# A PSUM bank written ahead by ScalarE, and a second diagonal product, in the last group of an edge-gated graph kernel

## The chip, the cores and the metric

One core of one Trainium2 chip runs the whole program in one launch. The metric is the device time of an execution in microseconds (us). The engines are named as the profile names them: PE (TensorE, matrix products; PEld is its weight load), DVE (VectorE), ACT (ScalarE), POOL (GpSimd, which here issues the gathers), SP (SyncE, which issues most other DMAs). SBUF is the on-chip memory that all engines read; PSUM holds the results of products, in banks of 512 fp32 values per partition.

## The reference

`x` is 16 batches of 1024 vertices with 256 features, and `adj` is a sparse 1024 x 1024 matrix (an edge with probability near 0.008, and the diagonal). Cut to what matters, with h = x:

```python
pre_u = h @ W1[:d]; pre_v = h @ W1[d:]
S   = sigmoid(relu(pre_u[u] + pre_v[v] + b1) @ W2 + b2)     # one number per edge (u, v) and batch
a_t = einsum('buv,bud->bvd', S * adj, h)
m_t = einsum('uv,bud->bvd', adj, h) * h
z_t = beta1*h + beta2*(a_t @ Wa + ba) + beta3*(m_t @ Wm + bm)
```

The kernel computes S for the edges alone. `z_t` is the output, and the change concerns how its first term, beta1 h, is added.

## The kernel before, in words

**Tiling.** The vertices v are cut into 8 tiles of 128, the batches into 4 groups g of 4. A pair (g, vt) is a *block*; there are 32, numbered k = 0 to 31 (`order`, L409), and the last group, g = 3, is blocks 24 to 31. A block's edges lie in 10 slots of up to 128 edges; one slot is one *step* n, so there are 320 steps, and s = n mod 10 is the step within its block.

**One step.** POOL gathers 128 rows of 8 KB from `table[g]`, which holds h W1[:d] and h side by side (`fetch`, L515; eight places, `fetched`). PE spreads pre_v over the slot's edges into a PSUM bank pair `pc` (`expand`, L610: two products, issued two steps ahead). DVE adds `pc` to the gathered rows (`add`, L646, one 128x1024 operation, for step n+1), then runs four `scalar_tensor_tensor` with an accumulator for step n (`gate`, L649), which give each edge's score. ACT makes the sigmoid (`gt`, L659) and scales the selection matrices `left` with it (L661). PE multiplies `left` with the gathered h rows into the accumulators `acc` (`aggregate`, L664); this frees the gathered tile, and POOL fetches the next one. At odd steps two slots are aggregated, at even ones none.

**One block's end.** When half of a 64-vertex window is done, ACT copies the accumulator to SBUF (`half_end`, L681), PE transposes it into a bank `misc` (`turn_over`, L691, four transposes) and ACT copies the result to `LT` (L694). For block k this stands in steps 8 and 9 of block k and in steps 0 and 2 of block k+1. DVE multiplies the `m` part with h (L705). Then `block_end(k)` runs in steps 4 to 7 of block k+1, one part to a step, each half (two batches) having two parts:

- steps 4 and 5, first half: a bank `pz` gets the bias row (L719, L449), then eight products with `w_a` in step 4 and eight with `w_m` in step 5 (L722). ACT copies `pz` to SBUF (L736), over the part of `LT` that is used up. One step later DVE makes hb = beta1 hb + z in one `scalar_tensor_tensor` (L737), and one step after that SP sends hb out (L739).
- steps 6 and 7, second half: the same products; in groups 0 to 2 also the same copy and DVE operation. In the last group (`h == 1 and g == NG - 1`, L724) PE adds beta1 h itself: two fp32 products with `be1_eye`, the diagonal matrix of beta1 (L726; the profile counts four, as fp32 goes in two passes). ACT then copies `pz` straight to hb (L728) and SP sends it (L730).

`halves(k+1)` (L473), in steps 1, 3, 4, 6 and 7 of block k, makes pre_v for the next block: a bias row and eight products into a bank (L480, L481), which ACT copies twice, to `X` and to `low` (L482, L483), one half in step 1, the other in step 3; then three copies between halves of the partitions (L486, L489).

**Banks.** `small()` (L220) hands out the two banks of the pool `psm` in turn, to `halves`, `turn_over`, `block_end` and, in the earlier groups, to the rows of the table and the edge lists. A tile that gets a bank waits until the readers of the bank's last tile are done. Block 31 is ended by `tail` (L753).

**Order of the work.** The order on each engine is that in which the program calls (`manual_schedule`, L492). `after(step, f)` puts f in front of the products of a later step. From step `LAST` = 230 on, `expand` and `products` come behind the gate of their step.

Of the kernel before, what the change touches and what calls it, by code (L numbers as in the profile page):

```python
# [7 lines left out]
FP = mybir.dt.float32  # L8
FR = mybir.dt.float32r
I32 = mybir.dt.int32  # L10
AF = mybir.ActivationFunctionType
ALU = mybir.AluOpType
AX = mybir.AxisListType
P = 128
# [3 lines left out]
def kernel(  # L18
# [42 lines left out]
    nc = tc.nc  # L61
    B, N, D = x.shape
    NT = N // P
    DC = D // P
    GB = 4
    NG = B // GB
# [22 lines left out]
    def load_rows(src, n, name, engine=nc.scalar, at_=None):  # L89
        t = const.tile([P, n], FP, name=name) if at_ is None else at_  # L90
        engine.dma_start(t, bass.AP(tensor=src.tensor, offset=src.offset, ap=[[0, P], [1, n]]))
        return t
# [8 lines left out]
    def fixed(shape, name, dt=FP):  # L101
        return const.tile(shape, dt, name=name)
# [90 lines left out]
    bias_p = fixed([P, D], "bias_p", FR)  # L193
# [12 lines left out]
    main = ctx.enter_context(ExitStack())  # L206
# [8 lines left out]
    lst = lst.enter_context(tc.tile_pool(name="lst", bufs=1))  # L215
    psc = main.enter_context(tc.tile_pool(name="psc", bufs=2, space=bass.MemoryType.PSUM))
    psa = main.enter_context(tc.tile_pool(name="psa", bufs=1, space=bass.MemoryType.PSUM))
    psm = main.enter_context(tc.tile_pool(name="psm", bufs=2, space=bass.MemoryType.PSUM))

    def small(name):  # L220
        return psm.tile([P, 512], FP, name="misc")


    def aside(vt):
        return psc.tile([P, GD], FP, name="pc") if vt < EARLY - 1 else small("pl")
# [176 lines left out]
    def after(step, f):  # L402
        due.setdefault(step, []).append(f)
# [38 lines left out]
    def half_product(p, hT, wt, h, begun):  # L442
        for bb in range(2):
            for i in range(DC):
                nc.tensor.matmul(p[:, bb * D:(bb + 1) * D], hT[:, 2 * h + bb, i, :], wt[:, i, :],  # L445
                                 start=(i == 0 and not begun), stop=(i == DC - 1), skip_group_check=begun)

    def add_row(p, parts):
        nc.tensor.matmul(p, unit, parts.unsqueeze(1).to_broadcast([P, 2, D]),  # L449
                         start=True, stop=False, skip_group_check=True)  # L450

    def rows(k, tab=None):

        g, nt = k
        for h in range(2):
            step = yield
            c = slice(2 * h * D, (2 * h + 2) * D)
            p = small("p")
            half_product(p, hTs[k], w_u, h, False)
            t = big.tile([P, 2 * D], FP, name=f"tab{h}", bufs=1) if tab is None else tab[:, c]  # L460
            nc.scalar.copy(t, p)
            if h == 1 and k in again:
                drop_hT(k)
            if tab is None:
                after(step + 1, lambda t=t, c=c: nc.sync.dma_start(table[g][nt * P:(nt + 1) * P, c], t))
        if tab is not None:
            after(step + 1, lambda: nc.sync.dma_start(table[g][nt * P:(nt + 1) * P, :GD], tab))

    cuts = {}

    def halves(k):  # L473
        X = cuts[k] = big.tile([P, NW, GD], FR, name="X")
        low = one.tile([P, GD], FP, name="low")
        for h in range(2):
            step = yield
            c = slice(2 * h * D, (2 * h + 2) * D)
            p = small("p")
            add_row(p, b1_p)  # L480
            half_product(p, hTs[order[k]], w_v, h, True)  # L481
            nc.scalar.copy(X[:, 0, c], p)  # L482
            nc.scalar.copy(low[:, c], p)  # L483
        after(step + (2 if k else 1), lambda: nc.vector.tensor_tensor(low, low, X[:, 0, :].bitcast(FP), ALU.subtract))  # L484
        yield
        nc.scalar.copy(X[W:, 1, :], X[W:, 0, :].bitcast(FP))  # L486
        for w in range(NW):
            yield
            nc.scalar.copy(X[(1 - w) * W:(2 - w) * W, w, :], low[w * W:(w + 1) * W])  # L489
# [56 lines left out]
    marks, pcs, accs, evs, hbs, LTs, lefts = {}, {}, {}, {}, {}, {}, {}  # L546
# [10 lines left out]
    m = 0  # L557
    piece = None
    parts = halves(0)
    for t, turns_ in enumerate(script):  # L560
        step = t - 100
# [148 lines left out]
    def block_end(k):  # L710

        g, vt = order[k]
        hb = hbs[k]
        for h in range(2):
            for i, wt in ((1, w_a), (0, w_m)):
                step = yield
                if i:
                    pz = small("pz")
                    add_row(pz, bias_p)  # L719
                for bb in range(2):  # L720
                    for c in range(DC):
                        nc.tensor.matmul(pz[:, bb * D:(bb + 1) * D], LTs[k][:, 2 * h + bb, i if bb else 1 - i, c, :], wt[:, c, :],  # L722
                                         start=False, stop=(i == 0 and c == DC - 1), skip_group_check=True)
            if h == 1 and g == NG - 1:  # L724
                for bb in range(2):
                    nc.tensor.matmul(pz[:, bb * D:(bb + 1) * D], be1_eye[0], hb[h][:, bb, :], start=False, stop=True,  # L726
                                     skip_group_check=True)
                nc.scalar.copy(hb[h], pz.rearrange("p (b d) -> p b d", b=2))  # L728
                b = g * GB + 2 * h
                after(step + 2, lambda hb=hb[h], b=b: nc.sync.dma_start(  # L730
                    out[b:b + 2, vt * P:(vt + 1) * P, :].rearrange("b p d -> p b d"), hb))
                continue
            z = pz.rearrange("p (b d) -> p b d", b=2)
            if step >= ROOM:
                z = LTs[k][:, 2 * h].rearrange("p k c n -> p (k c n)").rearrange("p (b d) -> p b d", b=2)
                nc.scalar.copy(z, pz.rearrange("p (b d) -> p b d", b=2))  # L736
            after(step + 1, lambda hb=hb[h], z=z: nc.vector.scalar_tensor_tensor(hb, hb, be1, z, ALU.mult, ALU.add))  # L737
            b = g * GB + 2 * h
            after(step + 2, lambda hb=hb[h], b=b: nc.sync.dma_start(  # L739
                out[b:b + 2, vt * P:(vt + 1) * P, :].rearrange("b p d -> p b d"), hb))  # L740
        del hbs[k], LTs[k]
# [79 lines left out]
    def products(n, k, s):  # L821
# [5 lines left out]
        if z <= s < z + 4 and 0 < k < BS:  # L827
            if s == z:
                end = block_end(k - 1)
                next(end)  # L830
            go(end, n)
# [20 lines left out]
        if k + 1 < BS and s - later in (0, 2, 3, 5, 6):  # L852
            if s == later:
                parts = halves(k + 1)
                next(parts)
            go(parts, n)
# [5 lines left out]
    ROOM, MORE, LISTS = 10, 3, 110  # L862
    LAST = (BS - NT - 1) * T
# [18 lines left out]
    for n in range(total + 2):  # L882
        k, s = divmod(n, T)
# [25 lines left out]
        if n == 1:  # L909
            bias = load_rows(bm, D, "bias", nc.sync, spare[:, 1])  # L910
            ba_b = load_rows(ba, D, "ba_b", nc.sync, spare[:, 2])
            be1 = load_rows(beta1, 1, "be1", nc.sync)
# [3 lines left out]
        if s in (5, 7) and k < BS - 1:  # L916
            h = s // 7
            hb = big.tile([P, 2, D], FP, name="h_blk", bufs=4)
            hbs.setdefault(k, []).append(hb)
            g, vt = order[k]  # L920
# [33 lines left out]
    with tc.If(any_left > 0):  # L954
        with ExitStack() as s2:
# [4 lines left out]
            for vt in range(NT):  # L960
                hb = fb.tile([P, B, D], FP, name="fb_h")
# [16 lines left out]
                f = fb.tile([P, 2 * GD], FP, name="fb_f")  # L978
# [3 lines left out]
                with tc.For_i(0, n_turns, 1):  # L982
# [9 lines left out]
                    for g in range(NG):  # L992
                        nc.gpsimd.indirect_dma_start(
                            out=f, out_offset=None, in_=table[g],
# [21 lines left out]
                for b in range(B):  # L1016
# [6 lines left out]
                    pz = fps.tile([P, D], FP, name="fb_pz")  # L1023
                    for k, w in enumerate((w_m, w_a)):
                        for c in range(DC):
                            nc.tensor.matmul(pz, lt[:, k, c, :], w[:, c, :],
                                             start=(k == 0 and c == 0), stop=(k == 1 and c == DC - 1))
# [34 lines left out]
```

## Time and profile before

| what | us |
|---|---|
| median of 3 runs | 1075.63 |
| the three runs | 1077.29, 1075.63, 1071.70 |
| the profiled execution's own time | 1082.24 |
| its span, first to last instruction | 1080.4 |
| busy: PE, DVE, ACT, POOL | 1020.1, 1017.6, 862.6, 459.3 |

The profile is one execution. A row of the timeline gives the start, the duration, the engine, the line of the kernel, the operation, what it writes and reads, and how many instructions are merged. Successive fp32 products overlap: their rows last 379 ns each and start 215 or 216 ns apart, so the distance between starts is what one costs the next. DVE's and ACT's rows overlap in a like way by some 0.07 to 0.12 us. Step 256 (s = 6 of block 25) is where DVE's L737 starts at 885.00 us; the following L737 start at 913.23, 941.42, 969.62, 997.86, 1026.05 and 1053.07, one in each block.

### The profile page before, as it was taken

The numbers are of one execution on the slowest core, as the hardware profiler recorded it, in microseconds if no ns is written. First come the engines' busy times: TensorE is split into PE (matmuls) and PEld (weight loads), VectorE is DVE, ScalarE is ACT, GpSimd is POOL, SyncE is SP. The second block draws the span as 40 slices with busy tenths as digits, with TensorE's granted clock in tenths as the row PEclk, the third lists the DMA queues.
The fourth block names the chain that finished last, engine by engine and source line by source line (L and its number), as shares of the span: only waits on it lengthen the run. The fifth ranks groups of instructions, "written<-read, shape, count | busy, mean of one in ns | idle before, by whom it ended". The sixth has DMA issues, their size and how long they took to land.

```text
span 1080.4 us, 24120 instructions
## 1 busy us (share of the span) xinstructions
PE 1020.1 (94%) x7673; PEld 731.3 (68%) x7673; DVE 1017.6 (94%) x3481; ACT 862.6 (80%) x2616; POOL 459.3 (43%) x456
## 2 busy tenths in 40 slices
PE   7777999999999999999999999999999999999996
PEld 6654676776666776677777767777766667666654
DVE  8687999998999999999999999999999999999993
ACT  3246787788888887898888888889889889999983
POOL 2666676555257334553333334333333333333330
PEclk9989999999999999999999999999999999999999
DMA  9999899999999999999999999999999999999991
GB/s 283 327 340 385 313 339 381 362 382 378 403 352 371 408 381 385 379 403 395 404 393 399 412 384 392 408 396 389 381 361 370 369 348 368 365 381 369 365 341 44
DMA packets 147752, 394.56 MB, mean 365 GB/s; under 512 B 18224, under 2 KB 94512, under 8 KB 111408
## 3 DMA queue, kind: packets, MB, share of 16 engines
q0 software_dynamic: 50544, 301.16, 70.9%
q1 hardware_dynamic: 83776, 78.66, 22.9%
q10 hardware_dynamic: 13296, 13.11, 3.5%
q8 instruction: 63, 1.03, 0.4%
q14 instruction: 73, 0.60, 0.1%
HBM read 396.93 MB, written 50.33 MB: 414 GB/s over the span
## 4 chain that ended last, share of the span: by engine, by line
PE 40%; DVE 34%; issue 10%; ACT 8%; DMA 5%; POOL 2%; another core or an unknown queue 0%; POOLq 0%; DVEq 0%; ACTq 0%
DVE fetched L656 16%; DVE fetched L648 12%; PE acc L673 10%; PE misc L722 10%; PE misc L445 9%; PE pc L615 7%; DMA fetched<-table,uidx 3%; PE misc L691 2%; ACT left L661 2%; DVE LT L705 1%; ACT X L489 1%; PE misc L449 1%; DVE low L484 1%; DVE h_blk L737 1%; DMA hT__635<-in_xT_dram 1%
## 5 line engine op out<-in xcount | busy, mean ns | idle before, releaser
L518 POOL DMA_INDIRECT fetched<-table,uidx x320 | 339.4, 1061 | 529.0 <-PE acc L673 389.0
L656 DVE SCALAR_TENSOR_TENSOR fetched<-fetched,w_b 128x256 f32<-128x256 f32 x1280 | 478.0, 419 | 0.0
L648 DVE TENSOR_TENSOR fetched<-fetched,pc 128x1024 f32<-128x1024 f32 x320 | 387.7, 1212 | 29.9 <-PE pc L615 19.4
L661 ACT ACTIVATE left<-left,gt 128x32 f32<-128x32 f32 (+1 forms) x1280 | 299.6, 305 | 10.4
L673 PE MATMUL acc<-fetched,left 128*32 128x256 f32 x4096 | 273.4, 385 | 6.3 <-ACT gt L659 3.7
L615 PE MATMUL pc<-X,mark 128*128 128x512 f32 x640 | 243.7, 462 | 10.9 <-DVE fetched L648 9.3
L673 PEld LDWEIGHTS acc<-fetched,left 128*32 128x32 f32 x4096 | 127.6, 109 | 112.1 <-issue 29.1
L615 PEld LDWEIGHTS pc<-X,mark 128*128 128x128 f32 x640 | 105.4, 189 | 88.9 <-issue 41.6
L659 ACT ACTIVATE gt<-sc,b_b 128x4 f32<-128x4 f32 x320 | 95.9, 300 | 46.7 <-DVE fetched L656 37.5
L722 PE MATMUL misc<-w_m,LT 128*128 128x256 f32 x496 | 117.3, 379 | 0.0
L722 PE MATMUL misc<-w_a,LT 128*128 128x256 f32 x496 | 117.2, 379 | 0.0
L445 PE MATMUL misc<-w_v,hT 128*128 128x256 f32 x448 | 107.6, 383 | 0.0
L722 PEld LDWEIGHTS misc<-w_a,LT 128*128 128x128 f32 x496 | 93.8, 189 | 15.3 <-issue 0.4
L722 PEld LDWEIGHTS misc<-w_m,LT 128*128 128x128 f32 x496 | 93.8, 190 | 15.1
L625 ACT ACTIVATE left<-onehot,val 128x64 f32<-128x64 bf16 (+1 forms) x320 | 102.9, 322 | 0.0
L385 POOL DMA_INDIRECT val<-in_adjT_dram,vidx x80 | 87.2, 1090 | 34.4 <-issue 20.4
L656 DVE DVE_READ_ACCUMULATOR fetched<-fetched,w_b 128x1 f32 x1280 | 100.7, 79 | 0.0
L691 PE MATMUL misc<-ident,ev 128*128 128x128 f32 x512 | 79.5, 278 | 18.5 <-issue 7.0
L445 PEld LDWEIGHTS misc<-w_v,hT 128*128 128x128 f32 x448 | 86.4, 193 | 14.3
L691 PEld LDWEIGHTS misc<-ident,ev 128*128 128x128 f32 x512 | 60.7, 141 | 45.7 <-ACT ev L681 15.2
L482 ACT CAST X<-misc 128x512 fp32r<-128x512 f32 x64 | 37.1, 580 | 55.2 <-PE misc L445 48.0
L445 PE MATMUL misc<-w_u,hT 128*128 128x256 f32 x320 | 76.6, 386 | 4.0 <-issue 3.8
(185 smaller groups left out, 1011.3 us busy)
## 6 DMA issues: line engine op xcount, KB each, us to landing
h_blk<-table SPq DMA_DIRECT2D x62, 256.0 KB
out_dram<-h_blk SPq DMA_DIRECT2D x62, 256.0 KB
hT<-in_xT_dram SPq DMA_DIRECT2D x28, 512.0 KB
table<-in_x_dram ACTq DMA_DIRECT2D x24, 512.0 KB
table<-tab SPq DMA_DIRECT2D x48, 256.0 KB
fetched<-table,uidx POOLq DMA_INDIRECT x320
table<-in_x_dram SPq DMA_DIRECT2D x8, 512.0 KB
table<-fetched SPq DMA_DIRECT2D x8, 512.0 KB
```

Of the source, the lines that this page charges most:

```text
L385: nc.gpsimd.indirect_dma_start(out=val[:, i, j:j + 1], out_offset=None, in_=adj_flat, in_offset=bass.IndirectOffsetOnAxis(ap=vidx[:, i, j: ...
L445: nc.tensor.matmul(p[:, bb * D:(bb + 1) * D], hT[:, 2 * h + bb, i, :], wt[:, i, :], start=(i == 0 and not begun), stop=(i == DC - 1), skip ...
L518: nc.gpsimd.indirect_dma_start(out=fetched[at_slot[n]], out_offset=None, in_=table[g], in_offset=bass.IndirectOffsetOnAxis(ap=uidx[:, vt * ...
L615: nc.tensor.matmul(pcs[n][:, c], marks[n // TW][:, j * P:(j + 1) * P], cuts[k][:, w, c], start=True, stop=True)
L625: nc.scalar.activation(lefts[n][:, :m, 1::GB, :], onehot[:, i, o:o + m, :].unsqueeze(2).to_broadcast([P, m, GB // 2, V]), AF.Copy, scale=v ...
L648: nc.vector.tensor_tensor(t, t, pcs.pop(n), ALU.add)
L656: nc.vector.scalar_tensor_tensor(t[:, b, :], t[:, b, :], 0.0, w2_b, ALU.max, ALU.mult, accum_out=sc[:, b:b + 1])
L659: nc.scalar.activation(gt, sc, AF.Sigmoid, bias=b2_b)
L661: nc.scalar.activation(lefts[n][:, :m, 2 * b, :], lefts[n][:, :m, 1 + b // 2 * GB, :], AF.Copy, scale=gt[:, b:b + 1])
L673: nc.tensor.matmul(accs[h][b * 2 * V:(b + 1) * 2 * V, r, :], left[:, i, 2 * b - b % 2:2 * b - b % 2 + 2].rearrange("p k v -> p (k v)"), f[ ...
L691: nc.tensor.transpose(pt[:, r, :, c, :], ev[:, r, c * P:(c + 1) * P], ident)
L722: nc.tensor.matmul(pz[:, bb * D:(bb + 1) * D], LTs[k][:, 2 * h + bb, i if bb else 1 - i, c, :], wt[:, c, :], start=False, stop=(i == 0 and ...
```

## The change

The two banks of `psm` get names, and `small` takes a wish for one of them. A new function `seed_z`, called from step 230 on behind the second half of `halves`, takes the bank that this half has just used, keeps it in a list `kept`, and has ACT write beta1 h of the block that ends next (`be1` as the scale) into it. While a bank is kept, `small` hands out the other. `block_end` takes a kept bank for the second half. What `small`, `seed_z`, `halves` and `block_end` get, cut to its core:

```diff
-    psm = main.enter_context(tc.tile_pool(name="psm", bufs=2, space=bass.MemoryType.PSUM))
-    def small(name):
-        return psm.tile([P, 512], FP, name="misc")
+    psm = main.enter_context(tc.tile_pool(name="psm", bufs=1, space=bass.MemoryType.PSUM))
+    turn_of, kept = [0], []
+    def small(name, bank=None):
+        if bank is None:
+            bank = turn_of[0] = 1 - turn_of[0]
+            if kept and kept[0][0] == bank:
+                bank = turn_of[0] = 1 - bank
+        return psm.tile([P, 512], FP, name=f"misc{bank}")
...
-    def add_row(p, parts):
+    def add_row(p, parts, start=True):
...
-                         start=True, stop=False, skip_group_check=True)
+                         start=start, stop=False, skip_group_check=True)
...
+    def seed_z(k, step):
+        bank = turn_of[0]
+        pz = small("pz", bank)
+        kept.append((bank, pz))
+        def write():
+            z, hb = pz.rearrange("p (b d) -> p b d", d=D), hbs[k][1]
+            if step >= LAST:
+                nc.scalar.activation(z, hb, AF.Copy, scale=be1)
...
             nc.scalar.copy(low[:, c], p)
+            if h == 1 and k > 1 and (step >= LAST):
+                seed_z(k - 2, step)
...
                 if i:
-                    pz = small("pz")
-                    add_row(pz, bias_p)
+                    filled = h == 1 and kept
+                    pz = kept.pop()[1] if filled else small("pz")
+                    if not filled or step >= LAST + 6:
+                        add_row(pz, bias_p, not filled)
...
-            if h == 1 and g == NG - 1:
+            by_eye = g == NG - 1 and not filled
+            if by_eye:
                 for bb in range(2):
                     nc.tensor.matmul(pz[:, bb * D:(bb + 1) * D], be1_eye[0], hb[h][:, bb, :], start=False, stop=True,
                                      skip_group_check=True)
+            if by_eye or filled:
                 nc.scalar.copy(hb[h], pz.rearrange("p (b d) -> p b d", b=2))
...
+            else:
+                z = pz.rearrange("p (b d) -> p b d", b=2)
+                if step >= ROOM:
+                    z = LTs[k][:, 2 * h].rearrange("p k c n -> p (k c n)").rearrange("p (b d) -> p b d", b=2)
+                    nc.scalar.copy(z, pz.rearrange("p (b d) -> p b d", b=2))
+                after(step + 1, lambda hb=hb[h], z=z: nc.vector.scalar_tensor_tensor(hb, hb, be1, z, ALU.mult, ALU.add))
```

(The left-out lines of `block_end` are those that send hb out; they stand behind both branches.)

More of the change, by code (lines that the diff above doesn't have):

```diff
@@ L467, in rows @@
             after(step + 1, lambda: nc.sync.dma_start(table[g][nt * P:(nt + 1) * P, :GD], tab))
+    def seed_z(k, step):
[7 more added lines that the diff above has]
+            else:
+                nc.vector.scalar_tensor_tensor(z, hb, be1, bias.unsqueeze(1).to_broadcast([P, 2, D]), ALU.mult, ALU.add)
+        if step >= LAST:
+            write()
+        else:
+            after(step + 1, write)
     cuts = {}
@@ L727, in block_end @@
                                      skip_group_check=True)
+            b = g * GB + 2 * h
+            if by_eye or filled:
                 nc.scalar.copy(hb[h], pz.rearrange("p (b d) -> p b d", b=2))
[L729 to L738, printed above, removed]
+            else:
+                z = pz.rearrange("p (b d) -> p b d", b=2)
[3 more added lines that the diff above has]
+                after(step + 1, lambda hb=hb[h], z=z: nc.vector.scalar_tensor_tensor(hb, hb, be1, z, ALU.mult, ALU.add))
             after(step + 2, lambda hb=hb[h], b=b: nc.sync.dma_start(
```

## The prediction

> **What bounds the kernel now.** I read the page's slices first (PE and DVE at 9 tenths nearly throughout), then the busy time by stretches, since the change acts only from step 230 on.
>
> ```profile
> 740.00:780.00 40.00, 39.87 (x319) 28.94 (x320) 37.59 (x126) 35.85 (x113) 14.53 (x14) 1.00 1.01 379
> 860.00:900.00 40.00, 38.19 (x318) 26.18 (x319) 40.00 (x134) 36.48 (x116) 14.14 (x14) 1.00 0.95 355
> 940.00:980.00 40.00, 38.77 (x326) 27.16 (x328) 40.00 (x137) 36.70 (x112) 14.40 (x14) 1.00 0.97 361
> ```
>
> The columns are the stretch, then PE, PEld, DVE, ACT, POOL, the granted clock, DMA. Before about 820 us PE is the full engine, later DVE: 40.00 of 40. A block lasts 28.22 us there (L737 at 885.00, 913.23, 941.42). PE looks to have 1.2 to 1.8 us left in 40, and where they lie decides, so I went through the timeline of block 24's end, PE first:
>
> ```profile
> 880.38 1.89 PE L722 MATMUL misc<-w_m,LT 128*128 128x256 f32 x8
> 881.92 0.82 PE L615 MATMUL pc<-X,mark 128*128 128x512 f32 x2
> ...
> 886.20 1.89 PE L722 MATMUL misc<-w_m,LT 128*128 128x256 f32 x8
> 887.92 1.03 PE L726 MATMUL misc<-h_blk,be_eye 128*128 128x256 f32 x4
> 888.60 0.81 PE L615 MATMUL pc<-X,mark 128*128 128x512 f32 x2
> 889.25 0.60 PE L691 MATMUL misc<-ident,ev 128*128 128x128 f32 x4
> 889.78 1.93 PE L673 MATMUL acc<-fetched,left 128*32 128x256 f32 x32
> 891.64 0.73 PE L615 MATMUL pc<-X,mark 128*128 128x512 f32 x2
> 892.21 0.60 PE L691 MATMUL misc<-ident,ev 128*128 128x128 f32 x4
> 892.56 0.70 PE L615 MATMUL pc<-X,mark 128*128 128x512 f32 x2
> 893.87 0.66 PE L691 MATMUL misc<-ident,ev 128*128 128x128 f32 x4 [0.60 <-ACT LT L694]
> ```
>
> Each row starts where the one above lets it, except the last: 0.57 us after L615 (as at 891.64 to 892.21) it could start at 893.13, so PE stands 0.74 us. A second stop, 0.26, is in the 24 products of L673 in step 3 (899.41 to 901.10, 1.69 us, where the same 24 take 1.43 at 894.46): they wait for ACT's `left`. So PE stands 1.0 us in 28.22 and has 27.2 us of work. ACT and DVE at the same place:
>
> ```profile
> 889.71 0.56 ACT L728 COPY h_blk<-misc 128x512 f32<-128x512 f32 x1
> ...
> 905.92 0.58 ACT L483 COPY low<-misc 128x512 f32<-128x512 f32 x1
> 907.17 0.30 ACT L659 ACTIVATE gt<-sc,b_b 128x4 f32<-128x4 f32 x1 [0.67 <-DVE fetched L656]
> ```
>
> ```profile
> 885.00 0.74 DVE L737 SCALAR_TENSOR_TENSOR h_blk<-h_blk,be,LT 128x512 f32<-128x512 f32 x1
> 885.66 1.21 DVE L648 TENSOR_TENSOR fetched<-fetched,pc 128x1024 f32<-128x1024 f32 x1
> ...
> 893.21 1.21 DVE L648 TENSOR_TENSOR fetched<-fetched,pc 128x1024 f32<-128x1024 f32 x1
> ```
>
> L737 holds DVE for 0.66 us (885.00 to 885.66). The add at 893.21 uses the `pc` that PE ends at 891.64 + 0.73 = 892.37: PE is only 0.84 us ahead here, the least of the block (the add at 885.66 has 2.9).
>
> **What the change does.** `filled` is not a flag: for the second half it is the list `kept` itself. `kept.pop()` empties that list, and an empty list counts as false in the two tests that follow. So the bias row is made with start=True, which overwrites what ACT wrote, and `by_eye` is true for both halves. In the built program the order on PE agrees: both halves of blocks 24 to 30 end with the diagonal product, and blocks 22 and 23 keep their DVE operation. What changes is this:
>
> - PE: seven more diagonal products (first halves of blocks 24 to 30). One costs four starts of 215.5 ns, 0.86 us; as a check, L722 to L615 takes 2.40 with it (886.20 to 888.60) and 1.54 without (880.38 to 881.92).
> - DVE: seven L737 fewer, 7 x 0.66 = 4.6 us.
> - ACT: eight seeds (blocks 22 to 29), whose result is never used. The first half's copy stays in its place and writes hb.
> - Banks: the kept bank does not advance the turn, so the transposes of step 8 get the bank that the second half's sum has just used, not the other one. They must wait for ACT's copy L728. This holds for blocks 22 to 29.
>
> **The seeds.** No row shows ACT writing PSUM. The nearest, ACT's copies of 128x512 out of PSUM, last 0.56 to 0.59 us; a copy within SBUF of 1024 a partition (L489) lasts 1.04. A seed starts after L483, at 906.50 + 0.03, and ACT then idles until 907.17. At 0.59 (taken, the same size) it ends 0.05 us before the gate: free. At 1.04 the gates of step 4 come 0.4 us late; if nothing covered that, 8 x 0.4 = 3.2 us. A gain is excluded, as the result is overwritten. [...]
>
> **The path, for each of the six blocks 24 to 29.** The second half's sum ends at 887.92 + 1.03 = 888.95; the new product of step 5 moves that by 0.86 to 889.81. ACT, free at 889.71, starts its copy 0.03 later, 889.84, and ends it 0.59 later, 890.43. The transposes start 0.05 after that, 890.48, not 889.25: 1.23 us late, 0.86 from the product and 0.37 from the bank. (0.03, 0.59 and 0.05 are from the end of block 30, where L726 ends at 1058.83, L728 runs from 1058.86 to 1059.45 and L691 starts at 1059.50.) Then L673 and L615 follow without a gap: `pc` is ready at 893.60 and DVE's add can start 0.04 later, 893.64 in place of 893.21. **DVE loses 0.43 us**, and the 0.66 us that it saved at 885.00 turn into idle time ahead of this add. Does the loss come back? PE's stops of 0.74 and 0.26 take up 1.00 of its 1.23. But from that add DVE works without a gap to its gates, ACT waits for them, and PE waits in step 3 for ACT's `left`, so PE is 0.43 us late as well when step 4 comes, and the round repeats: 28.22 becomes 28.65. Six blocks: 2.6 us.
>
> **The other places.** Blocks 22 and 23 have no new product, only the bank: their step 8 transposes would start 1.94 us late (block 23: copy ends 861.40, transposes were at 859.52). The add behind has 2.35 us in hand (862.64 to 864.99), and PE's stops there come to some 2 us: 0. Block 30 has no seed. Its new product lies on PE's chain to the end, which from 1043.68 on is PE nearly alone in the chain of waits; the 32 products at 1053.18, which take 2.40 in place of 1.93 as they wait for `left`, give part back: 0.39 to 0.86, I take 0.6. Queues: aggregations behind the transposes come 1.2 us later, and with them POOL's fetches (they wait for PE, 4 to 5 us at a time). A fetch issued at 892.45 is used at 904.55, and DMA falls to 98 GB/s at 880 to 881, between two pairs, so it has run dry: 0. If that cover failed, 6 x (1.23 - 0.43) = 4.8 us more. SP's sends of hb keep their places, and their data is there sooner.
>
> **Sum:** 2.6 + 0.6 = 3.2 us slower. The profiled execution took 1082.24 (span 1080.4), so 1085.4 by it; the median of the runs is 6.6 below it, and I forecast 1075.63 + 3.2 = 1078.8.
>
> [...]
>
> **Rivals.**
> 1. *The bank costs nothing* (ACT copies sooner, or the wait falls on time in which PE stood). Then PE is 0.86 late, against 0.84 - 0.04 of cover: 0.06 a block, 0.4, and 0.6 at the end: +1, 1076.6. Against it: L691 at 1059.50 waits for L728 in just this way.
> 2. *DVE's time is the time* (faster): seven L737 leave and PE follows: -4.6, 1071.0. It would need PE's products to fit into stops other than the 1.0 us a block that I see; 7 x 0.86 = 6.0 us must fit into 7.
> 3. *All of the bank's wait lands on the end* (slower): 6 x 1.23 + 2 x 1.94 + 0.86 = 12.1 us, 1087.7. The mechanism is PE's delay at the step 8 transposes handed on in full. It decides once PE has no stop left between step 9 and step 3, that is, once the 0.74 and 0.26 us vanish because ACT slips with PE. Half of it gives 1081.7. For it: ACT is 36.5 of 40 busy and idles little between steps 6 and 9.
>
> **Numbers.** Forecast 0.58, rival 1 0.15, rival 2 0.07, rival 3 0.20. This kernel's measurement tells about 0.5%, 5.4 us, from no change. Rival 2 is mostly inside that (0.04 beyond); rival 3 mostly outside, and with the seeds' 3.2 us added to the forecast slower gets 0.23. Within 0.5%: 0.73. The range goes from rival 2 to about half of rival 3 with the seeds' upper end: 1071.5 to 1084.5.
>
> **What would show it.** Right: blocks of about 28.65 us; a DVE that idles about 1.1 us ahead of the add behind step 9; the step 8 transposes waiting for ACT's copy in each block; eight ACT rows that write `misc`, near 0.59 us, each ending before the gate. Wrong: blocks shorter than 28.2 (rival 2), no wait of those transposes (rival 1), blocks over 29 us (rival 3), or seeds near 1 us with late gates.

## The result, and the profile after

The changed kernel takes 1088.41 us (median of 8 runs, 1083.89 to 1094.91), the kernel before 1076.19 beside it (8 runs, 1071.70 to 1080.40): ratio 1.0106, 95% interval 1.0072 to 1.0140. That is 12.2 us slower by the medians; the forecast was 3.2, and its range ended at 1084.5.

The profiled execution of the changed kernel is the highest of its 8 (1094.91, span 1093.1), and that of the kernel before (1082.24) lies above its eight runs, so the stages count for more than the totals. In the changed kernel the add is L671, `expand` L638, the gate L679, the transposes L714, the block's products L747, the diagonal product L752, ACT's copy to hb L756, the seed L484 and the aggregation L696. First the busy times by stretches, 11 us later than those shown of before (stretch, PE, PEld, DVE, ACT, POOL, granted clock, DMA):

```profile
751.00:791.00 40.00, 39.86 (x322) 28.62 (x321) 37.81 (x125) 35.99 (x113) 15.02 (x15) 1.00 1.01 380
871.00:911.00 40.00, 39.79 (x337) 27.81 (x336) 39.07 (x132) 36.62 (x113) 15.69 (x15) 1.00 0.97 355
951.00:991.00 40.00, 39.57 (x326) 28.04 (x328) 38.05 (x130) 36.75 (x112) 14.13 (x14) 1.00 0.97 351
```

In the last group DVE, full before with 40.00 of 40, now has 1 to 2 us idle. PE stands less: 40 us hold one and a half blocks, so how many of its stops fall in depends on where the stretch is cut, but over 880 to 1020 us it is busy 138.93 us of 140, where it was 136.87 before. The end of block 24 on PE:

```profile
896.22 1.89 PE L747 MATMUL misc<-w_m,LT 128*128 128x256 f32 x8
897.95 1.03 PE L752 MATMUL misc<-h_blk,be_eye 128*128 128x256 f32 x4
898.63 0.81 PE L638 MATMUL pc<-X,mark 128*128 128x512 f32 x2
899.65 0.66 PE L714 MATMUL misc<-ident,ev 128*128 128x128 f32 x4 [0.21 <-ACT h_blk L756]
900.24 1.93 PE L696 MATMUL acc<-fetched,left 128*32 128x256 f32 x32
902.10 0.74 PE L638 MATMUL pc<-X,mark 128*128 128x512 f32 x2
```

ACT's seed of this block and its next gate, and the copy that the transposes wait for:

```profile
887.43 0.69 ACT L484 ACTIVATE misc<-h_blk,be 128x512 f32<-128x512 f32 x1
888.07 0.30 ACT L682 ACTIVATE gt<-sc,b_b 128x4 f32<-128x4 f32 x1
...
899.01 0.59 ACT L756 COPY h_blk<-misc 128x512 f32<-128x512 f32 x1
```

And DVE's add behind step 9:

```profile
902.88 1.22 DVE L671 TENSOR_TENSOR fetched<-fetched,pc 128x1024 f32<-128x1024 f32 x1 [0.80 <-PE pc L638]
```

This is the forecast's picture: the diagonal product still there, the transposes waiting for the copy (it ends 899.60, they start 899.65), a `pc` that comes late, and DVE idle where it had been full.

But this is not where most of the time went. Cut at DVE's adds of steps 230 and 255 (times from the timelines, to the end of the span):

| stage | before, us | after, us |
|---|---|---|
| step 230 to the end | 276.6 | 281.4 |
| of it steps 230 to 255 | 72.4 | 73.7 |
| one block, mean of the six from step 251 to 311 | 28.21 | 28.72 |

The last group lost 4.8 us; the rest of the 12.7 between the spans was lost before step 230. There the view of waits (engine, line, whom it waited for: us in total, times, longest) has lines for 60 to 500 us that the kernel before does not have in this size; L305 is `from_` in the edge lists, DVE's last read of the list's small product `pw`:

```profile
PEld misc L450 <- DVE from L305: 8.2, 2, 5.6
PE misc L450 <- DVE from L305: 7.3, 2, 5.2
PEld misc L714 <- DVE from L305: 5.6, 1, 5.6
PE misc L714 <- DVE from L305: 5.1, 1, 5.1
```

The longest wait for `from_` in the kernel before is 0.6 us on PE and 1.0 on its weight load. The cause is in the pool. The front part says that `small()` hands out the two banks in turn; compared by the banks that the two programs use, the old pool does not. Among the 260 tiles up to step 230 it gives the same bank twice running at nine places, from the 37th tile to the 124th, while edge lists are being made (the last list's `from_` is read at 406 us): a list's `pw` then holds the other bank while DVE works through a chain of small operations. The new `small()`, which counts turns itself, alternates without exception, and hands PE the bank that `pw` still holds.

### The profile page after: what moved, and what is told of

It is laid out like the page before. It is cut to its first block, busy times and chain, and to the rows that moved or that the text cites. A ratio compares the mean times of both kernels' runs of the same rounds, so it can differ in the third digit from the quotient of the medians.

```text
span 1093.1 us, 24198 instructions
## 1 busy us (share of the span) xinstructions
PE 1027.1 (94%) x7701; PEld 742.1 (68%) x7701; DVE 1015.8 (93%) x3474; ACT 867.5 (79%) x2624; POOL 458.6 (42%) x456
## 4 chain that ended last, share of the span: by engine, by line
PE 59%; DVE 17%; ACT 9%; DMA 9%; issue 4%; POOL 1%; SPq 0%; DVEq 0%; POOLq 0%; ACTq 0%
PE acc L696 15%; PE misc L747 14%; PE misc L450 13%; PE pc L638 9%; DVE fetched L679 7%; DVE fetched L671 5%; PE misc L714 3%; DMA hT<-in_xT_dram 3%; ACT left L684 3%; DMA fetched<-table,uidx 2%; PE misc L454 2%; DMA key<-in_adjT_dram 2%; ACT X L512 2%; PE misc L752 1%; ACT LT L761 1%
## 5 line engine op out<-in xcount | busy, mean ns | idle before, releaser
L541 POOL DMA_INDIRECT fetched<-table,uidx x320 | 336.0, 1050 | 542.4 <-PE acc L696 401.0
L679 DVE SCALAR_TENSOR_TENSOR fetched<-fetched,w_b 128x256 f32<-128x256 f32 x1280 | 480.3, 424 | 0.0
L671 DVE TENSOR_TENSOR fetched<-fetched,pc 128x1024 f32<-128x1024 f32 x320 | 389.3, 1216 | 42.6 <-PE pc L638 34.1
L696 PE MATMUL acc<-fetched,left 128*32 128x256 f32 x4096 | 270.6, 386 | 2.8 <-ACT left L684 2.5
L638 PE MATMUL pc<-X,mark 128*128 128x512 f32 x640 | 244.9, 464 | 14.6 <-DVE fetched L671 14.5
L696 PEld LDWEIGHTS acc<-fetched,left 128*32 128x32 f32 x4096 | 127.3, 110 | 105.8 <-issue 26.1
L638 PEld LDWEIGHTS pc<-X,mark 128*128 128x128 f32 x640 | 106.2, 191 | 92.1 <-issue 32.1
L747 PE MATMUL misc<-w_m,LT 128*128 128x256 f32 x496 | 117.3, 379 | 0.0
L747 PE MATMUL misc<-w_a,LT 128*128 128x256 f32 x496 | 117.2, 379 | 0.0
L679 DVE DVE_READ_ACCUMULATOR fetched<-fetched,w_b 128x1 f32 x1280 | 106.7, 83 | 0.0
L747 PEld LDWEIGHTS misc<-w_a,LT 128*128 128x128 f32 x496 | 93.8, 189 | 15.3 <-ACT LT L717 0.4
L747 PEld LDWEIGHTS misc<-w_m,LT 128*128 128x128 f32 x496 | 93.8, 190 | 15.1
L714 PE MATMUL misc<-ident,ev 128*128 128x128 f32 x512 | 80.6, 281 | 14.7 <-DVE from L305 5.1
L714 PEld LDWEIGHTS misc<-ident,ev 128*128 128x128 f32 x512 | 62.7, 144 | 40.7 <-ACT ev L704 11.8
L717 ACT COPY LT<-misc 128x512 f32<-128x512 f32 x128 | 73.1, 571 | 7.7 <-PE misc L714 7.7
```

The lines of the kernel that those rows point to most:

```text
L541: nc.gpsimd.indirect_dma_start(out=fetched[at_slot[n]], out_offset=None, in_=table[g], in_offset=bass.IndirectOffsetOnAxis(ap=uidx[:, vt * ...
L638: nc.tensor.matmul(pcs[n][:, c], marks[n // TW][:, j * P:(j + 1) * P], cuts[k][:, w, c], start=True, stop=True)
L671: nc.vector.tensor_tensor(t, t, pcs.pop(n), ALU.add)
L679: nc.vector.scalar_tensor_tensor(t[:, b, :], t[:, b, :], 0.0, w2_b, ALU.max, ALU.mult, accum_out=sc[:, b:b + 1])
L696: nc.tensor.matmul(accs[h][b * 2 * V:(b + 1) * 2 * V, r, :], left[:, i, 2 * b - b % 2:2 * b - b % 2 + 2].rearrange("p k v -> p (k v)"), f[ ...
L714: nc.tensor.transpose(pt[:, r, :, c, :], ev[:, r, c * P:(c + 1) * P], ident)
```

## The experiments

Each kernel was run with the kernel before on the same chip. The median of before differs from chip to chip (1074.86 to 1076.33, and 1082.07 for the last two runs), so ratios carry the verdicts; a ratio is not the quotient of the two medians and differs from it by up to 0.15%. "From step 230 on" and "per block" are from one profile each, as in the table above; in that profile before has 276.6 and 28.21.

My theory was that the loss has two parts: strict turns of the banks, before step 230, and what the forecast described, in the last group. Its rival was that the last group's delays are handed on in full, about 12 us, as in the prediction's rival 3. The letters in the expectations are those of each run's own text.

### Strict turns alone

```diff
-    psm = main.enter_context(tc.tile_pool(name="psm", bufs=2, space=bass.MemoryType.PSUM))
+    psm = main.enter_context(tc.tile_pool(name="psm", bufs=1, space=bass.MemoryType.PSUM))
+    turn_of = [0]
     def small(name):
-        return psm.tile([P, 512], FP, name="misc")
+        bank = turn_of[0] = 1 - turn_of[0]
+        return psm.tile([P, 512], FP, name=f"misc{bank}")
```

> The kernel before with nothing but the two named banks handed out strictly in turn; no seed, no second diagonal product. Theory A (the loss lies in the last group): no change, within 0.3%, and the time from the add of step 230 to the end as before, 276.5 us. Theory B (most of the loss comes from the other order of the banks while the edge lists are made, ahead of step 230): 6 to 9 us slower, with PE waiting some 5 us at a time for DVE's operations on the lists, and 276.5 us from step 230 on.

Measured: 1082.83 against 1076.33, ratio 1.0061 (1.0038 to 1.0084); from step 230 on 276.2. So over half of the loss comes from an edit that touches no operation. The places, from the timeline of PE in this run (L302 is `from_` here):

```profile
179.53 0.81 PE L617 MATMUL pc<-X,mark 128*128 128x512 f32 x2
185.44 3.78 PE L447 MATMUL misc<-w_u,hT__1791 128*128 128x256 f32 x8 [5.10 <-DVE from L302]
...
275.87 0.73 PE L617 MATMUL pc<-X,mark 128*128 128x512 f32 x2
281.73 1.12 PE L693 MATMUL misc<-ident,ev 128*128 128x128 f32 x4 [5.13 <-DVE from L302]
...
404.39 3.64 PE L447 MATMUL misc<-w_u,hT 128*128 128x256 f32 x8 [2.83 <-DVE from L302]
```

PE stands for 13.1 us in these three places, and the eight products behind a wait last 3.78 and 3.64 us where such eight last 1.89: PE comes back at half speed. The changed kernel stops at the first of these places too (5.17 us, the eight products 3.78), and the clock granted there is 0.56 from 185 to 190 us. By the medians 6.5 us of this reach the end. A single profile does not show that sum: up to the add of step 230 there are 802.1 us here and 803.9 in the profile of before, whose execution was 6 us above its median, 797.0 to 801.6 in the seven runs below that keep the old order up to there, and 804.6 and 804.9 in the last two, on a slower chip. So the medians and the waits carry the 6.5 us, and the 7.9 us that the profiles of before and after lie apart there are as uncertain.

### The change, with the banks up to step 230 in the old order

```diff
+    early = list("1010...")      # the old kernel's order, written out up to step 230
     def small(name, bank=None):
+        if bank is None and early:
+            turn_of[0] = bank = int(early.pop(0))
```

> The changed kernel, but up to step 230 with the bank order of the kernel before, written out as a list. Theory A: 10 to 13 us slower than before, like the changed kernel. Theory B: only what the last group loses in the profile of the changed kernel, 3.5 to 5 us, all of it behind step 230: 276.5 becomes 280 to 281.5.

Measured: 1080.07, ratio 1.0050 (1.0026 to 1.0074); from step 230 on 280.0, per block 28.71, and of the waits for `from_` one of 0.6 us, as in the kernel before. The last group costs 3.4 us from step 230 on, 3.7 by the medians, against the forecast's 3.2; the ratio gives 5.4, its interval 2.8 to 8.0. The two parts, 0.61% and 0.50%, make up the 1.06% of the change within the intervals; by the medians they are 6.5 and 3.7 of 12.2 us. That the last group's delays are handed on in full falls.

### A second diagonal product alone

```diff
-            if h == 1 and g == NG - 1:
+            if g == NG - 1:
```

> The kernel before with the diagonal product for both halves of blocks 24 to 30, seven DVE operations fewer; no seeds, banks as before. The working of the prediction without the bank: 0.06 us a block and 0.6 at the end, +1 us; blocks of 28.2 to 28.3 us. If DVE's time were the time: -4.6 us. If the extra product lands on the end in full: +6 us.

Measured: 1078.47, ratio 1.0015 (0.9990 to 1.0040); from step 230 on 277.3, per block 28.28. Seven operations of 0.66 us left DVE, seven products of 0.86 us came to PE, and a block is 0.07 us longer: the forecast's rival 1 had put that at 0.06. The agreement is in part luck, as PE is now busy 140.00 us of 140 (second fence of "First halves by DVE again"): the block is PE's whole work, 28.28 us, where the forecast's 27.2 + 0.86 makes 28.06; PE had some 0.2 us a block less to spare than it counted.

### The turn set when the kept bank is taken

On top of the change with the old early order:

```diff
                     filled = h == 1 and kept
+                    if filled:
+                        turn_of[0] = kept[0][0]
                     pz = kept.pop()[1] if filled else small("pz")
```

> The second kernel of this call with one line more: taking the kept bank counts as a turn, so the transposes of step 8 get the bank that has been free since step 5. The eight seeds, whose result is overwritten, and the second diagonal product stay. If the bank's wait costs what the prediction says, this gives it back: blocks of 28.2 to 28.3 us in place of 28.7, 3 to 4 us faster than the second kernel, about +1 against before. If the seeds or the product cost it, no change against the second kernel.

Measured: 1078.20, ratio 1.0022 (0.9996 to 1.0049); from step 230 on 277.7, per block 28.32. The transposes of step 8 get the other bank, and 2.3 us of 3.4 come back (0.39 us a block). What stays, 0.4 us more than with two diagonal products alone, is all that the eight dead seeds can cost by these profiles.

### beta1 h used, with the turn set

Now the second half's sum keeps what ACT wrote, so only the first half takes a diagonal product:

```diff
-                    filled = h == 1 and kept
+                    filled = h == 1 and bool(kept)
```

> The change, with the banks before step 230 in the old kernel's order, with filled a plain true or false taken before the list is popped (so that the second half's sum keeps beta1 h that ScalarE wrote, its bias row adds to it, and only the first half takes the diagonal product), and with the turn set to the kept bank when the sum takes it. Seven diagonal products of 0.86 us leave against the run with the turn advanced, one per block stays as in the kernel before, and DVE does none of the last group's updates. Theory A (PE's string of products sets the block, and the dead seed with its second diagonal product cost about what that run showed): from step 230 to the end 276 to 277.7 us, no more than the 277.7 of the run with the turn advanced and no less than the 276.6 of the kernel before, less up to 0.5; whole time 0 to +1.5 us against the kernel before (ratio 0.998 to 1.002). Theory B (DVE is a bound of the blocks: its 0.66 us of update per block leaves the path): from step 230 to the end 272 us, 4.6 less than the kernel before, ratio near 0.996.

Measured: 1071.61 against 1076.03, ratio 0.9973 (0.9944 to 1.0002); from step 230 on 272.5, per block 27.68. Its theory A, mine, missed; its theory B, with DVE as a bound, holds. 1.4 us of the gain lie in steps 230 to 255, where the second halves of blocks 22 and 23 now need no DVE update. Once more, on another chip:

> The same kernel as the run with beta1 h used and the turn advanced, once more, beside the run before in this call, for a narrower interval against the kernel before: from step 230 on 272.5 us within 0.3 as in its first profile; ratio 0.995 to 0.999. If its first ratio of 0.997 was chance, about 1.000, and the 4.1 us of the last group then come back as a loss before step 230.

Measured: 1072.53 against 1074.86, ratio 0.9976 (0.9951 to 1.0001); from step 230 on 271.8, per block 27.63. Both profiles gain 4.1 to 4.8 us in the last group. Over the whole each interval ends at 1.000: some 0.25% faster, just at the edge of what is measured.

### beta1 h used, the turn not set

> As the run before in this call, but the turn stays as the change has it, so that the transposes of step 8 get the bank of the second half's sum and wait for ScalarE's copy. Theory A: the wait costs what it cost between the two earlier runs that differ in the turn alone (280.0 against 277.7 from step 230 on, 2.3 us), less what the shorter string of products makes of it: from step 230 to the end 277 to 279.5 us, ratio 1.001 to 1.004. Theory B (the second diagonal product is what makes the wait matter): no difference from the run with the turn advanced, within 0.5 us from step 230 on.

(The same without the `turn_of[0] = kept[0][0]` lines.) Measured: 1081.06, ratio 1.0040 (1.0018 to 1.0062); from step 230 on 280.5, per block 28.47. Both theories missed: from step 230 on the run takes not 2.3 us more than the one with the turn set, but 8.0. Of these, 0.8 lie in each of the six blocks and 2.4 in blocks 22 and 23 (1.6 of them in a stretch at half clock, below); 0.9 is a wait of DVE for a gathered tile at 1044 us, which has no shown link to the bank. The bank is seen in the waits of 820 to 1072 us (L717 are the transposes here, L759 ACT's copy to hb), where the run with the turn set has one wait of 0.5 on PEld and 0.2 on PE:

```profile
PEld misc L717 <- ACT h_blk L759: 12.5, 9, 2.2
PE misc L717 <- ACT h_blk L759: 8.8, 9, 1.8
```

Why the wait grew shows in one block of this run, PE and then ACT:

```profile
884.65 0.82 PE L641 MATMUL pc<-X,mark 128*128 128x512 f32 x2
886.31 0.66 PE L717 MATMUL misc<-ident,ev 128*128 128x128 f32 x4 [0.84 <-ACT h_blk L759]
```

```profile
884.27 0.30 ACT L685 ACTIVATE gt<-sc,b_b 128x4 f32<-128x4 f32 x1
884.60 0.96 ACT L687 ACTIVATE left<-left,gt 128x32 f32<-128x32 f32 x4
885.46 0.33 ACT L651 ACTIVATE left<-onehot,val 128x64 f32<-128x64 bf16 x1
885.70 0.56 ACT L759 COPY h_blk<-misc 128x512 f32<-128x512 f32 x1
```

The sum is done when the row at 884.65 starts or soon after, but ACT copies it only at 885.70, behind three groups of its own step. The wait ends at ACT's time; a product less on PE mostly makes it longer, and the block, 28.47, is only 0.24 us shorter than that of the change with the old early order.

### beta1 h used, strict turns throughout

The changed kernel with the `bool(kept)` edit alone.

> The changed kernel with one edit: filled is a plain true or false, so that ScalarE's write is used. The banks are strictly in turn from the first step, as the change has it. Theory A (the loss lies mostly before step 230, in the order of the banks): slower than the kernel before by the 6.5 us that the banks alone cost, plus or minus 2.5, plus 0.5 to 3 in the last group, +4.5 to +12 us, ratio 1.004 to 1.011; PE waits two or three times some 5 us for the list operations of DVE before step 130, and from step 230 to the end it takes the same as the run before in this call, within 1 us. Theory B (the loss is the dead write and its second diagonal product): within 2 us of the kernel before, ratio 0.998 to 1.002.

Measured: 1084.71, ratio 1.0074 (1.0038 to 1.0110); per block 28.47, from step 230 on 277.9. Theory A holds: using beta1 h does not mend the kernel. The stretch from step 230 on is 2.6 us shorter than in the run above instead of equal within 1: the blocks are equal to the hundredth, 1.6 us of the difference is the stretch at half clock in that run, which this one escaped, and 0.9 that run's wait for a gathered tile.

### First halves by DVE again

beta1 h used and the turn set, and:

```diff
-            by_eye = g == NG - 1 and not filled
+            by_eye = g == NG - 1 and h == 1 and not filled
```

> The run with beta1 h used and the turn advanced, but with the first half of the last group's blocks updated by DVE, as in the kernel before, and not by the diagonal product: per block PE has 0.86 us less and DVE 0.66 us more than in that run. What is told apart: what bounds the last group's blocks, 28.2 us each in the kernel before and 27.65 with the turn advanced and beta1 h used. Theory A (PE and DVE both set the block, since each waits for the other in turn; by the earlier runs 0.66 us of DVE is worth 0.58 and 0.86 us of PE 0.66): from the kernel before, PE's product goes and DVE stays, 28.2 - 0.66 = 27.55 per block, 272 us from step 230 on, ratio 0.994 to 0.998. Theory B (DVE alone sets the block, PE's product is covered): 28.2 per block again, 276.6 from step 230 on, ratio 0.999 to 1.002. Theory C (PE alone): 27.65 - 0.86 = 26.8 per block, 267 from step 230 on.

Measured: 1074.24 against 1074.86, ratio 1.0003 (0.9975 to 1.0032); per block 28.19, from step 230 on 274.8 (of the 1.8 less than 276.6, 1.4 are those of blocks 22 and 23). Theory B: with PE relieved of 0.86 us a block, the block is the 28.2 us of the kernel before. One line of 860 to 1000 us each, in the columns of above, of this run, of the one with two diagonal products alone, and of the one with beta1 h used and the turn set:

```profile
860.00:1000.00 140.00, 133.96 (x1072) 94.07 (x1074) 140.00 (x467) 130.61 (x399) 51.05 (x50) 1.00 0.97 364
```

```profile
860.00:1000.00 140.00, 140.00 (x1106) 100.57 (x1099) 137.72 (x465) 126.38 (x391) 50.01 (x49) 1.00 0.98 363
```

```profile
860.00:1000.00 140.00, 138.10 (x1107) 98.60 (x1106) 139.79 (x473) 131.97 (x407) 52.41 (x52) 1.00 0.99 370
```

In the first DVE is busy 140.00 of 140 and PE idles, in the second it is the other way round, in the third both are close to full. So a block lasts as long as the longer of two full engines: DVE 28.2 with its update and at most 27.65 without, PE 28.28 with two diagonal products and at most 27.65 with one.

### Strict turns that pass by the lists

Strict turns alone, and:

```diff
+    turn_of, listed = [0], []
...
+        if listed and listed[0] == bank:
+            bank = turn_of[0] = 1 - bank
...
-        return psc.tile([P, GD], FP, name="pc") if vt < EARLY - 1 else small("pl")
+        if vt < EARLY - 1:
+            return psc.tile([P, GD], FP, name="pc")
+        t = small("pl")
+        listed[:] = [turn_of[0]]
+        return t
...
         nc.vector.tensor_tensor(from_, pw[:, 3:4], from_, ALU.max)
+        listed.clear()
...
         pe = aside(vt)
+        listed.clear()
```

> The kernel before with the two banks named and strictly in turn, as in the run with named banks alone, but while the small product pw of an edge list lies in a bank, until DVE has read it for the last time (L299 of the kernel before), tiles get the other bank; the last steps and the rest are strictly in turn. Theory A (the 6.5 us that strict turns cost are the waits of PE for DVE's list operations, since a strict turn hands out a bank that such a product still holds): the three waits of some 5 us for DVE's tile from_ are gone, and the time is that of the kernel before, ratio 0.998 to 1.002. Theory B (naming the banks, or their order elsewhere, costs): as the run with named banks alone, ratio 1.004 to 1.008, with or without those waits.

Measured: 1082.99 against 1082.07, ratio 1.0003 (0.9980 to 1.0026). The waits of PE for `from_` (L308 here) in 60 to 500 us shrink to one:

```profile
PE misc L701 <- DVE from L308: 0.7, 1, 0.7
```

The interval's upper end, 1.0026, lies below the lower end of strict turns, 1.0038. That settles the first part: strict turns cost through the banks that a list's product holds.

### The change, mended in all three places

The changed kernel with `bool(kept)`, the turn set, and the rule for lists of the run above.

> The changed kernel with three edits of one to four lines: turns pass by a bank that holds a list's product, as in the run before in this call; filled is a plain true or false; the turn is set to the kept bank when the sum takes it. If the three costs found are all there are: as the run with beta1 h used and the turn advanced (0.9973 and 0.9976), ratio 0.995 to 1.000, blocks of 27.6 to 27.7 us, from step 230 on 272 to 272.6 us. If the written-out order of the banks did more than keep clear of the lists: 1.001 to 1.005, with the difference before step 230.

Measured: 1080.96 against 1082.07, ratio 0.9989 (0.9962 to 1.0016); from step 230 on 272.9, per block 27.80, both a little over what I expected. It agrees with 0.9973 and 0.9976 within the intervals, and 1.006 of strict turns is gone. Why its blocks are 0.15 us longer than in the other two runs was not followed up.

## Why the prediction was wrong

The step that failed stands in its first paragraph: **"the change acts only from step 230 on"**. The sum and every rival were built on it. The renamed pool acts from the first tile, and by the runs with strict turns alone (1.0061) and with the lists passed by (1.0003) it costs 6.5 us before step 230. The diff showed it: `bufs=2` under one name became a count of turns. I had taken from the code that the old pool alternates and did not compare the two programs' banks one after the other.

The rest, by its own steps:

- `filled` as the list itself, the dead seed, both halves by the diagonal product: right; the rows of block 24 above.
- A block at 28.65: measured 28.72, six blocks 3.06 us for 2.6. The parts agree, too: the product 0.06 (0.07 measured alone, in part by luck, as said there), the bank 0.37 (0.39 between the runs that differ in the turn).
- DVE idle "about 1.1" ahead of the add: 0.80.
- The end 0.6: 0.45 (35.35 against 34.9 from step 315 on). The seeds: 0.69 us each, not the 0.59 taken from the copies out of PSUM, and still without cost, 0.4 us for eight at most.
- Blocks 22 and 23 at 0: right except for one stretch at half clock, 1.33 us in the profiled execution, which no step foresaw.
- Rival 2, DVE's 4.6 us: did not happen, but DVE did bound the blocks before, and 4.1 to 4.8 us come back where PE keeps to one diagonal product and the bank is free (1.4 of them in steps 230 to 255, with the updates of blocks 22 and 23, which rival 2 did not count). In the kernel as changed the second product makes PE the bound at once: with two diagonal products alone PE was full, 28.28 us a block, while its weight loads were busy 100.57 us of 140.
- Rival 3 named 1087.7, close to 1088.41, but its mechanism did not happen: none of the six blocks over 29 us, and 3.4 us where it had 12.1.

Open: the changed kernel's profile lost 7.9 us before step 230, strict turns 6.5 by their median. One place of the profile that strict turns do not explain is a standstill of PE for a late load of `hT`, with half clock behind it (granted 0.50 from 515 to 520 us):

```profile
515.37 3.78 PE L450 MATMUL misc<-w_v,hT 128*128 128x256 f32 x8 [8.88 <-DMA hT<-in_xT_dram]
```

The kernel before has no such stop in its profile. But it does not come from the change: the run with two diagonal products alone, which up to block 24 is the kernel before, stops 4.6 us for the same load, and the six runs of the changed kernel with the old early order stop 2.5 to 8.9 us. Strict turns alone, the lists passed by and the kernel mended in all three places do not have it, and with strict turns and beta1 h used it is 0.7 us. What decides it was not tried.

## What to carry to other kernels

A buffer pool's order of reuse is part of the schedule, 6.5 us of it here: when a pool is replaced by a hand-written rotation, compare the two sequences of buffers from the first tile to the last, and look for tiles that are held long, before any cost in the edited stage is worked out. With two engines both full, moving work from one to the other gained nothing (blocks of 28.19 us with DVE's update, 28.28 with the second diagonal product); with the work gone from both they took 27.68, and ACT had the room, busy 131.97 us of 140. A wait that ended at a third engine's time swallowed most of what was saved ahead of it (0.86 us less on PE made the block 0.24 shorter): free the buffer first, then shorten the work.

## What was not expected of the hardware

A stop of 1.8 us was followed by PE at half clock in some executions and not in others. In block 22 of the changed kernel (first fence) and of the run with beta1 h used and strict turns (second fence) PE stops for the same 1.78 us:

```profile
840.44 0.66 PE L714 MATMUL misc<-ident,ev 128*128 128x128 f32 x4 [1.78 <-ACT LT L761]
841.02 3.34 PE L696 MATMUL acc<-fetched,left 128*32 128x256 f32 x32
```

```profile
831.34 0.66 PE L714 MATMUL misc<-ident,ev 128*128 128x128 f32 x4 [1.78 <-ACT h_blk L756]
831.93 1.93 PE L696 MATMUL acc<-fetched,left 128*32 128x256 f32 x32
```

The 32 products behind it last 3.34 us in the one and 1.93 in the other; the granted clock is 0.83 from 836 to 846 us in the first and 1.00 from 820 to 846 in the second. The run with beta1 h used and the turn not set has the same as the first (1.77 us, then 3.19; clock 0.72 from 827 to 833 us). In block 23 the changed kernel stops for 1.77 us at 870.64, and the 32 products behind it last 1.93; in the two other runs PE stands for 1.77 and 1.81 us of the 20 from 840 to 860, at a clock of 1.00. So two of these three runs came back at half clock in block 22, and none in block 23. Longer stops were not all followed by it: PE came back at full rate after 2.17 us in the changed kernel (at 405.20, eight products in 1.99 us) and after 2.20 us in the kernel before (at 188.53, 1.99 as well), and at half after 2.83 us with strict turns alone (at 404.39, 3.64). The length of a stop alone does not decide it in these profiles; what does was not shown.

The bank of a tile counts as well: with the step 8 transposes in the same bank as the sum before, a block was 0.39 us longer with the dead seed (28.71 against 28.32) and 0.8 with beta1 h used (28.47 against 27.68). That a rotation can also be too strict, when one bank is held, is what the 6.5 us show.
